# Two stacked graph-attention layers on one core: longer row-sum chains, one head's additions moved to adding transfers, and layer 1's transposes grouped

## The chip, the cores and the metric

The kernel runs on one core of one Trainium2 chip. A core has five engines that run side by side, each with its own queue in strict order: TensorE (PE, matrix products into PSUM; its weight loads are listed as PEld), VectorE (DVE), ScalarE (ACT), GpSimd (POOL) and SyncE (SP, which here only issues transfers). Sixteen DMA engines move data between HBM and SBUF, the on-chip memory. The metric is the device time of one execution in microseconds (us), as the median over runs.

## The reference

The input is x with 8 batches of 2048 nodes and 256 features, and one adjacency matrix adj of 2048 x 2048 for all batches. Two layers follow each other; each adds its result to its input and normalizes every row.

```python
# layer 0: 8 heads of 32 features; the prior is adj itself
x_proj = einsum('bnd,hdf->bhnf', x, W)
e = leaky_relu(e_src[..., :, None] + e_dst[..., None, :], 0.2)
e = e + beta * log(adj + 1e-6)
e = where(adj > 0, e, -inf)
h = softmax(e) @ x_proj
x = layernorm(x + concat_heads(h) @ W_out.T)
# layer 1: one head, dot-product scores
h1, h2, h3 = x @ W1, x @ W2, x @ W3
e = where(adj > 0, leaky_relu(h1 @ h2.T, 0.2), -1e12)
x = layernorm(x + relu(softmax(e) @ h3))
```

All is in 32-bit floating point. In layer 0 a score depends on a source and a destination value only, so the exponential of the score can be written as a product of factors of the row and the column and the larger of two terms; the mask times the prior is one matrix for all batches and heads.

## The kernel before, in words

The kernel is one long program without loops on the chip. Nodes are cut into NT = 16 row tiles of P = 128. Tiles of 128 x 2048 of 32-bit numbers ("wide" tiles) take 8 KB of each partition.

Layer 0 (class `Gat`). Heads go in NP = 4 pairs of HP = 2. One unit of work is one pair and one row tile `jt` (method `step`, 64 units per batch). For each of the two heads, DVE makes a wide tile `s` of unnormalized, transposed attention weights in one instruction (L375): the larger of the column row `c` and a per-partition factor `re`, times the mask matrix's tile `mt`. `mt` comes from DRAM, where batch 0 put it (`load_mt`, L202), into a pool of two buffers. PE then multiplies `s` by the head's values `v` and adds up over the 16 tiles in the PSUM tile `val`; four products, two heads by two halves of the columns, stand side by side in the array, each 32 columns wide (method `products`, L407).

The row sums of the softmax (the denominators) are needed too. For a tile in no chain, PE makes them by a second set of products with the same `s`, into the PSUM tile `den`; the weight operand is then the factor `e`, repeated 32 times. For the tiles of a chain (the table `SUMMED`, by batch and pair) PE leaves these out, and the sum is kept in SBUF, in one wide tile `d` for each head. The first tile of a chain starts `d` by a scaled copy on ACT (L392). Each later tile of the chain is added by one DVE instruction for each head (L386), one unit late: at unit jt the tile jt - 1 is added, after the `s` of unit jt. At the last unit PE multiplies both `d` by a block of ones into `den`, so a chain costs one tile's products at its end. Before the change, the chains hold 6 tiles in three pairs of batch 1; in batches 2 to 7 they hold 4 tiles in the first pair and 8 in each of the others. Batch 0 and the first pair of batch 1 have none.

Layer 1 (class `Dot`). A step takes one row tile: PE multiplies the queries by all keys (L538, four PSUM tiles `e`), ACT applies the leaky ReLU on the way out into the wide tile `p` (L540), DVE masks `p` and finds the row's extreme (L543), and ACT takes the exponential in place (L546). In the next step PE transposes `p` in four groups of four 128 x 128 blocks (function `turned`, L561), ACT copies each group to `pts` (L563), and PE multiplies by `h3` into the PSUM tile `acc` (L577). The last lines divide, add the residual and normalize. In the kernel before, the first group is transposed ahead of the next row tile's scores; the other three stand between the products, each one group ahead.

How the layers meet. For each batch, layer 0 of the next batch is woven into layer 1 of this one: `dot.step` calls `fill` at three places, and each call runs some layer-0 units. The order of PE's instructions is the order of the program text (`manual_schedule` for PE from the start, for SP from batch 1 on); the other engines' orders are set by a scheduler at build time. PSUM is full: `ps` has three buffers of one bank, shared by all short products ("mm" tiles), and `pacc` holds `val`, `den` and `acc`.

SBUF buffers that matter here, by tag: `s` 4, `mt` 2, `d` 2, `c` 3 and `p` 2 wide tiles; `pt` (the `pts`) 2 and `v` 3 small ones. In batch 0 the two `p` buffers also serve the first loads of x and the making of the mask matrix (`make_m`).

Of the kernel before, what the change touches and what calls it, by code (L numbers as in the profile page):

```python
# [27 lines left out]
def kernel(  # L28
# [36 lines left out]
    IG = BK // P  # L65


    SUMMED = [[()] * NP, [()] + [(0, 3, 6, 8, 11, 14)] * (NP - 1)]
    SUMMED += [[(2, 4, 10, 13)] + [tuple(range(0, NT, 2))] * (NP - 1)] * (B - 2)

    const = ctx.enter_context(tc.tile_pool(name="const", bufs=1))
    dram = ctx.enter_context(tc.tile_pool(name="dram", bufs=1, space=DRAM))
    whole = ctx.enter_context(tc.tile_pool(name="whole", bufs=1))
# [48 lines left out]
            nc.vector.tensor_mul(wa, wp[:, kc, 0:D], a_bc)  # L122
            nc.vector.tensor_reduce(dst[:, kc, :], wa.rearrange("p (h f) -> p h f", h=H), AX.X, ALU.add)

    first_x = [wide.tile([P, NT // 2, D], F32, tag="p", name="xr", bufs=2) for _ in range(2)]
    for g in range(NB):
        nc.sync.dma_start(first_x[g // 2][:, ts(g % 2, IG), :],
                          x[0].rearrange("(t p) d -> p t d", p=P)[:, ts(g, IG), :])
# [5 lines left out]
    def later_weights():  # L134

        nc.sync.dma_start(w3s, w3.rearrange("(k p) d -> p k d", p=P))
        w1t, w2t = (chunk.tile([P, KC, D], F32, tag="pt", name=name, bufs=2) for name in ("w1t", "w2t"))
        for w, dst in ((w_out, wot), (w1, w1t), (w2, w2t)):
            src = [row_tile("square") for _ in range(KC)]
            for o in range(KC):  # L140
                nc.sync.dma_start(src[o], w[ts(o, P), :])
            yield
            for kc in range(KC):
                t = mm_tile("sq_t")
                for o in range(KC):
                    nc.tensor.transpose(t[:, ts(o, P)], src[o][:, ts(kc, P)], ident)
                nc.scalar.copy(dst[:, kc, :], t[:, 0:D])
        yield
        for dc in range(KC):
            t = mm_tile("w12p")  # L150
            for kc in range(KC):
                nc.tensor.matmul(t[:, 0:D], w1t[:, kc, ts(dc, P)], w2t[:, kc, :], start=(kc == 0), stop=(kc == KC - 1))
            nc.scalar.copy(w12[:, dc, :], t[:, 0:D])
        yield
# [23 lines left out]
    def make_m(jt):  # L178

        a = wide.tile([P, NT, P], I32, tag="d", name="adj_t", bufs=2)  # L180
        nc.sync.dma_start(a, adj[:, ts(jt, P)].rearrange("(t p) j -> p t j", p=P))
        m = wide.tile([P, NT, P], F32, tag="p", name="m", bufs=2)
        nc.vector.tensor_scalar(m, a, 0.0, None, ALU.max)
        nc.scalar.activation(m, m, AF.Ln, bias=eps_prior)
        nc.scalar.activation(m, m, AF.Exp, scale=beta_c)
        nc.vector.scalar_tensor_tensor(m, a, 0.0, m, ALU.is_gt, ALU.mult)
        return m
# [46 lines left out]
    class Gat:  # L234
# [12 lines left out]
        def scores_first(self, xt):  # L247


            t = mm_tile("scores")  # L250
            for kc in range(KC):
                for q in range(NB):
                    nc.tensor.matmul(t[ts(q, DH), :], wp[:, kc, D:], xt[:, kc, ts(q, BK)],
                                     start=(kc == 0), stop=(kc == KC - 1))
            s = chunk.tile([P, BK], F32, tag="pt", name="scores", bufs=2)
            nc.scalar.copy(s, t)
            t = mm_tile("scores_t")
            for k in range(IG):
                nc.tensor.transpose(t[:, ts(k, P)], s[:, ts(k, P)], ident)
            nc.scalar.copy(self.both.rearrange("p (q k) h -> p k q h", k=IG),  # L260
                           t.rearrange("p (k q h) -> p k q h", k=IG, h=DH)[:, :, :, 0:2 * H])
# [38 lines left out]
            nc.sync.dma_start(c_d[self.b].rearrange("h (t p) -> (h t) p", p=P), est)  # L300

        def load(self, hp):
            self.v[hp] = chunk.tile([P, NT, HP * DH], F32, tag="v", name="v", bufs=3)
            nc.sync.dma_start(self.v[hp], v_d[self.b, hp])

        def load_factors(self):
# [33 lines left out]
        def step(self, count=1):  # L340

            for _ in range(count):
                hp, jt = next(self.units)
                for work in list(self.later):
                    if next(work, self) is self:
                        self.later.remove(work)
                if hp == NP - 1 and jt == 0 and self.b + 1 < B:
                    gats[self.b + 1].load_factors()

                at = self.b * NP + hp + 1  # L350
                if at < B * NP:
                    gat = gats[at // NP]
                    if jt == 4 and gat.b > 0:
                        gat.load(at % NP)
                    elif jt == 12:
                        gat.scale(at % NP)
                if jt == 0:
                    if self.b > 0:
                        self.cs = [self.cs_ahead.pop(0) for _ in range(HP)]
                    else:  # L360
                        self.cs = [self.query_rows(hp * HP + a) for a in range(HP)]
                    self.val = pacc.tile([P, HALF], F32, tag="val", name="val")
                    self.den = pacc.tile([P, HALF], F32, tag="den", name="den")
                first = self.b == 0 and hp == 0
                if first:
                    self.more_mt(jt + 2, jt > 0)
                if self.b > 0:
                    mt = self.mts.pop(0)
                else:
                    mt = self.mts[jt] if first else load_mt(jt, True)  # L370
                s = []
                for a in range(HP):
                    h = hp * HP + a
                    sa = wide_tile("s", "s", 4)
                    nc.vector.scalar_tensor_tensor(sa, self.cs[a], self.re[:, 0, jt, h:h + 1], mt, ALU.max, ALU.mult)  # L375
                    s.append(sa)
                    if self.b > 0 and jt == NT - 1:
                        self.cs_ahead += [c for c in [next(self.c_loads, None)] if c]
                if self.b > 0 and len(self.mts) < (4 if not SUMMED[self.b][hp] and jt < NT - 4 else 2):
                    self.mts += [t for t in [next(self.mt_loads, None)] if t]  # L380
                v, e = self.v[hp], self.re[:, 1]
                heads = [hp * HP + a for a in range(HP)]
                chain = SUMMED[self.b][hp]
                if jt - 1 in chain[1:]:
                    for d, sa, h in zip(self.sums, self.last, heads):
                        nc.vector.scalar_tensor_tensor(d, sa, e[:, jt - 1, h:h + 1], d, ALU.mult, ALU.add)  # L386
                self.last = s
                self.products(self.val, [v[:, jt, ts(a, DH)] for a in range(HP)], s, jt == 0, jt == NT - 1)
                if jt in chain[:1]:
                    self.sums = [wide_tile("d", "d", 2) for _ in heads]  # L390
                    for d, sa, h in zip(self.sums, s, heads):
                        nc.scalar.activation(d, sa, AF.Copy, scale=e[:, jt, h:h + 1])  # L392
                if jt not in chain:
                    self.products(self.den, [e[:, jt, h:h + 1].to_broadcast([P, DH]) for h in heads], s,
                                  jt == min(set(range(NT)) - set(chain)),
                                  not chain and jt == NT - 1)
                if chain and jt == NT - 1:
                    self.products(self.den, [ones] * HP, self.sums, False, True)
                if jt == NT - 1:
                    work = self.finish(hp)  # L400
                    next(work)
                    self.later.append(work)
# [112 lines left out]
    class Dot:  # L515
# [15 lines left out]

        def scores(self, it):
            pen = mask(it, self.b == 0)
            p = wide_tile("p", "p", 2)
            for c in range(NB):
                t = mm_tile("e")
                for kc in range(KC):
# [11 lines left out]
        def step(self, fill=lambda k: None):  # L549
# [8 lines left out]
            def turned(g):  # L558
                t = mm_tile("pt")
                for k in range(IG):  # L560
                    nc.tensor.transpose(t[:, ts(k, P)], p[:, ts(g * IG + k, P)], ident)  # L561
                pt = chunk.tile([P, BK], F32, tag="pt", name="pts", bufs=2)
                nc.scalar.copy(pt, t)  # L563
                return pt

            pt = turned(0)
            if it + 1 < NT:
                if (it + 1) % IG == 0:
                    self.queries((it + 1) // IG)
# [1 line left out]
            fill(1)  # L571
            acc = pacc.tile([P, D], F32, tag="acc", name="acc")
            for g in range(NB):
                now, pt = pt, turned(g + 1) if g + 1 < NB else None
                for k in range(IG):
                    j = g * IG + k
                    nc.tensor.matmul(acc, now[:, ts(k, P)], self.h3[:, j, :], start=(j == 0), stop=(j == NT - 1))  # L577
            fill(2)
            rec = small.tile([P, 1], F32, name="rec1", bufs=2)
            nc.vector.reciprocal(rec, den)  # L580
# [28 lines left out]
    def others():  # L609
# [18 lines left out]
        for n, (gat, g) in enumerate(groups):  # L628
            if g == 0:
                gat.begin()  # L630
            v = chunk.tile([P, NP, IG, HP * DH], F32, tag="v", name="v", bufs=3)
            for k in range(IG):
                gat.row(g * IG + k, xts[n], v[:, :, k, :])
                if k == 1:
# [103 lines left out]
```

The softmax here doesn't subtract the row's maximum and nothing guards it: scores larger than these inputs give would overflow.

## Time and profile before

The median of three runs is 4321.98 us (4317.75 to 4324.15). The profiled execution took 4317.4 us.

| engine | busy us | share | instructions |
|---|---|---|---|
| PE | 4191.7 | 97% | 24640 |
| PE weight loads | 2202.1 | 51% | 24640 |
| DVE | 3704.8 | 86% | 2468 |
| ACT | 1657.5 | 38% | 3019 |
| POOL | 9.5 | 0% | 14 |

| group | count | busy us | mean ns |
|---|---|---|---|
| DVE, score tiles `s` (L375) | 1024 | 2355.5 | 2343 |
| DVE, additions to `d` (L386) | 318 | 738.5 | 2342 |
| PE, values `val` (L407) | 8192 | 1024.5 | 602 |
| PE, denominators `den` of single tiles (L407) | 5216 | 664.1 | 597 |
| PE, layer 1 products `acc` (L577) | 4096 | 955.9 | 381 |
| PE, layer 1 scores `e` (L538) | 2048 | 904.0 | 594 |
| PE, layer 1 transposes `pt` (L561) | 2048 | 317.7 | 278 |
| ACT, starts of `d` (L392) | 54 | 107.9 | 2011 |

How to read it. Busy time is the time in which at least one instruction of the engine or group ran; on PE several run at once, so a mean of one instruction times its count is more than the busy time. A product of 32-bit numbers appears as two records. Some PE records are missing (5216 of 5648 of `den` are there). The transfers moved 843.50 MB, 195 GB/s on average; the largest part are 496 loads of `mt`, 1 MB each. In the steady part of the run one batch takes about 500 us.

### The profile page before, as it was taken

Reading aid. Unit: us, or ns where it says so; the run is one execution under the profiler, and the core shown is the slowest. Engines: PE = TensorE matmul, PEld = TensorE weight load, DVE = VectorE, ACT = ScalarE, POOL = GpSimd, SP = SyncE. Lnnn points to the kernel's source line nnn. Section 1 sums busy time; section 2 is a strip of 40 time slices with the busy share of each in tenths; the row PEclk is TensorE's granted clock in tenths of the full one; section 3 lists DMA queues with packets and bytes.
Section 4 is the critical chain, followed back from the end, with each engine's and each line's share of the span. In section 5 each row is a group of like instructions: output and inputs, shape, how many; then the busy total and the mean of one; then the engine's idle time right before and its main releaser. Section 6 shows DMA issues by size and latency. Waiting matters only on the chain. (4 is left out here: it accounts for less than half of the span.)

```text
span 4317.4 us, 58896 instructions
## 1 busy us (share of the span) xinstructions
PE 4191.7 (97%) x24640; PEld 2202.1 (51%) x24640; DVE 3704.8 (86%) x2468; ACT 1657.5 (38%) x3019; POOL 9.5 (0%) x14
## 2 busy tenths in 40 slices
PE   7999999999999999999999999999999999999999
PEld 5444455454454545544554544555455445545766
DVE  7878888998899989999899998999899998999222
ACT  7522233333333333333343334333333333433554
POOL 0000000000000000000000000000000000000000
PEclk9999999999999999999999999999999999999999
DMA  8979756666555554556555564555545565544211
GB/s 272 308 258 319 273 198 210 225 229 209 184 191 192 201 203 180 179 184 227 187 193 186 189 207 183 192 190 206 202 176 181 186 226 185 198 171 146 81 50 41
DMA packets 267946, 843.50 MB, mean 195 GB/s; under 512 B 32672, under 2 KB 165792, under 8 KB 193952
## 3 DMA queue, kind: packets, MB, share of 16 engines
q1 hardware_dynamic: 232352, 806.17, 53.0%
q10 hardware_dynamic: 35328, 33.56, 2.3%
q8 instruction: 193, 3.16, 0.3%
q14 instruction: 73, 0.60, 0.0%
HBM read 763.76 MB, written 75.37 MB: 194 GB/s over the span
## 5 line engine op out<-in xcount | busy, mean ns | idle before, releaser
L375 DVE SCALAR_TENSOR_TENSOR s<-c,re,mt 128x2048 f32<-128x2048 f32 x1024 | 2355.5, 2343 | 150.3 <-PE den L407 65.6
L407 PE MATMUL val<-s,v 128*32 128x512 f32 x8192 | 1024.5, 602 | 56.7 <-DVE s L375 56.5
L577 PE MATMUL acc<-h,pts 128*128 128x256 f32 x4096 | 955.9, 381 | 18.5 <-ACT pts L563 18.5
L538 PE MATMUL e<-x1t,h 128*128 128x512 f32 x2048 | 904.0, 594 | 4.6 <-ACT pts L563 4.5
L577 PEld LDWEIGHTS acc<-h,pts 128*128 128x128 f32 x4096 | 746.9, 190 | 119.4 <-ACT pts L563 34.2
L386 DVE SCALAR_TENSOR_TENSOR d<-s,re,d 128x2048 f32<-128x2048 f32 x318 | 738.5, 2342 | 0.0
L407 PE MATMUL den<-s,re 128*32 128x512 f32 x5216 | 664.1, 597 | 0.0
L538 PEld LDWEIGHTS e<-x1t,h 128*128 128x128 f32 x2048 | 379.0, 190 | 451.6 <-issue 413.5
L407 PEld LDWEIGHTS val<-s,v 128*32 128x32 f32 x8192 | 245.5, 110 | 675.0 <-issue 519.9
L563 ACT COPY pts<-pt 128x512 f32<-128x512 f32 x512 | 295.4, 582 | 663.5 <-PE pt L561 660.3
L540 ACT ACTIVATE p<-e 128x512 f32<-128x512 f32 x512 | 302.6, 595 | 426.1 <-PE e L538 412.7
L543 DVE CUSTOM_DVE_ANT_0 p<-p,pen 128x2048 f32<-128x2048 f32 x128 | 292.4, 2284 | 198.7 <-ACT p L540 198.6
L407 PEld LDWEIGHTS den<-s,re 128*32 128x32 f32 x5216 | 181.5, 111 | 396.4 <-issue 394.6
L561 PEld LDWEIGHTS pt<-ident,p 128*128 128x128 f32 x2048 | 238.5, 141 | 214.4 <-issue 173.9
L546 ACT ACTIVATE p<-p,neg 128x2048 f32<-128x2048 f32 x128 | 256.7, 2005 | 232.2 <-DVE neg L543 232.2
L561 PE MATMUL pt<-ident,p 128*128 128x128 f32 x2048 | 317.7, 278 | 0.0
L582 ACT ACTIVATE z<-acc,rec 128x256 f32<-128x256 f32 x128 | 60.7, 474 | 391.6 <-PE acc L577 259.4
L583 DVE TENSOR_TENSOR z<-z,x1r 128x256 f32<-128x256 f32 x128 | 53.8, 420 | 142.9 <-ACT z L582 142.8
L392 ACT ACTIVATE d<-s,re 128x2048 f32<-128x2048 f32 x54 | 107.9, 2011 | 80.0 <-PE den L407 66.3
L268 PE MATMUL proj<-wp,xt 128*128 128x272 f32 (+1 forms) x512 | 132.5, 404 | 4.8 <-ACT v L270 3.2
L528 PE MATMUL h1p<-x1t,w 128*128 128x512 f32 x256 | 117.0, 595 | 9.4 <-ACT x1t L503 9.4
L270 ACT COPY v<-proj 128x256 f32<-128x256 f32 x128 | 47.0, 375 | 202.5 <-PE proj L268 197.5
(88 smaller groups left out, 1919.8 us busy)
## 6 DMA issues: line engine op xcount, KB each, us to landing
mt<-mt_d SPq DMA_DIRECT2D x496, 1024.0 KB
c<-c_d SPq DMA_DIRECT2D x64, 1024.0 KB
pen<-pen_d SPq DMA_DIRECT2D x112, 512.0 KB
xg<-in_x_dram SPq DMA_DIRECT2D x60, 512.0 KB
adj_t<-in_adj_dram SPq DMA_DIRECT2D x16, 1024.0 KB
mt_d<-mt SPq DMA_DIRECT2D x16, 1024.0 KB
rb<-rec_d SPq DMA_DIRECT2D x128, 128.0 KB
x_d<-ht ACTq DMA_DIRECT2D x32, 512.0 KB
```

The costliest lines, as they stand in the source:

```text
L268: nc.tensor.matmul(t[:, 0:cols], xt[:, kc, ts(it % IG, P)], wp[:, kc, 0:cols], start=(kc == 0), stop=(kc == KC - 1))
L375: nc.vector.scalar_tensor_tensor(sa, self.cs[a], self.re[:, 0, jt, h:h + 1], mt, ALU.max, ALU.mult)
L386: nc.vector.scalar_tensor_tensor(d, sa, e[:, jt - 1, h:h + 1], d, ALU.mult, ALU.add)
L407: nc.tensor.matmul(dst[ts(q, DH), ts(c, BK)], weights[q % 2], s[q % 2][:, ds(q // 2 * HALF + c * BK, BK)], start=start, stop=stop)
L528: nc.tensor.matmul(t, w12[:, kc, ts(dc, P)], self.x1t[:, kc, ts(g, BK)], start=(kc == 0), stop=(kc == KC - 1))
L538: nc.tensor.matmul(t, self.h1[:, kc, ts(it % IG, P)], self.x1t[:, kc, ts(c, BK)], start=(kc == 0), stop=(kc == KC - 1))
L540: nc.scalar.activation(p[:, ts(c, BK)], t, AF.Prelu, alpha=ALPHA)
L543: nc.vector.tensor_tensor_reduce(p, p, pen, -1.0, FMAX, ALU.add, ALU.min, neg)
L546: nc.scalar.activation(p, p, AF.Exp, bias=neg, scale=-1.0, accum_out=den)
L561: nc.tensor.transpose(t[:, ts(k, P)], p[:, ts(g * IG + k, P)], ident)
L563: nc.scalar.copy(pt, t)
L577: nc.tensor.matmul(acc, now[:, ts(k, P)], self.h3[:, j, :], start=(j == 0), stop=(j == NT - 1))
```

## The change

It has two parts that share memory.

First, the chains get longer: 10 of 16 tiles (0, 1, 3, 4, 6, 7, 9, 10, 12, 14) in the three later pairs of batches 1 to 7, and 6 tiles (2, 4, 6, 8, 10, 12) in the first pair of batches 2 to 7. It is meant to take denominator products off PE. So that DVE needn't make all the additions, those of the pair's first head, for tiles up to BY_DMA = 12, are made otherwise: ACT writes the scaled tile into a wide tile `w` (one buffer), and a transfer issued by GpSimd adds `w` into `d`. The later tile 14, and all of the second head, stay on DVE.

Second, all four transposes of a row tile of layer 1 now stand together at the head of the step, ahead of the next row tile's scores. Then `p` is free before the next scores are written and needs one buffer, which makes room for `w`; the four `pts` need four buffers, which the third buffer of `v` makes room for. The first loads of x and `make_m` use the tags `p` and `w` in turn.

```diff
-    SUMMED = [[()] * NP, [()] + [(0, 3, 6, 8, 11, 14)] * (NP - 1)]
-    SUMMED += [[(2, 4, 10, 13)] + [tuple(range(0, NT, 2))] * (NP - 1)] * (B - 2)
+    SUMMED = [[()] * NP, [()] + [(0, 1, 3, 4, 6, 7, 9, 10, 12, 14)] * (NP - 1)]
+    SUMMED += [[(2, 4, 6, 8, 10, 12)] + [(0, 1, 3, 4, 6, 7, 9, 10, 12, 14)] * (NP - 1)] * (B - 2)
+    BY_DMA = 12
...
-    first_x = [wide.tile([P, NT // 2, D], F32, tag="p", name="xr", bufs=2) for _ in range(2)]
+    first_x = [wide.tile([P, NT // 2, D], F32, tag=tag, name="xr", bufs=1) for tag in "pw"]
...
-        m = wide.tile([P, NT, P], F32, tag="p", name="m", bufs=2)
+        m = wide.tile([P, NT, P], F32, tag="pw"[jt % 2], name="m", bufs=1)
...
-            self.v[hp] = chunk.tile([P, NT, HP * DH], F32, tag="v", name="v", bufs=3)
+            self.v[hp] = chunk.tile([P, NT, HP * DH], F32, tag="v", name="v", bufs=2)
...
                 if jt - 1 in chain[1:]:
                     for d, sa, h in zip(self.sums, self.last, heads):
-                        nc.vector.scalar_tensor_tensor(d, sa, e[:, jt - 1, h:h + 1], d, ALU.mult, ALU.add)
+                        if h == heads[0] and jt - 1 <= BY_DMA:
+                            w = wide_tile("w", "w", 1)
+                            nc.scalar.activation(w, sa, AF.Copy, scale=e[:, jt - 1, h:h + 1])
+                            nc.gpsimd.dma_start(d, w, accum_op=ALU.add)
+                        else:
+                            nc.vector.scalar_tensor_tensor(d, sa, e[:, jt - 1, h:h + 1], d, ALU.mult, ALU.add)
...
-            p = wide_tile("p", "p", 2)
+            p = wide_tile("p", "p", 1)
...
-                pt = chunk.tile([P, BK], F32, tag="pt", name="pts", bufs=2)
+                pt = chunk.tile([P, BK], F32, tag="pt", name="pts", bufs=NB)
...
-            pt = turned(0)
+            pts = [turned(g) for g in range(NB)]
...
-                now, pt = pt, turned(g + 1) if g + 1 < NB else None
                 for k in range(IG):
                     j = g * IG + k
-                    nc.tensor.matmul(acc, now[:, ts(k, P)], self.h3[:, j, :], start=(j == 0), stop=(j == NT - 1))
+                    nc.tensor.matmul(acc, pts[g][:, ts(k, P)], self.h3[:, j, :], start=(j == 0), stop=(j == NT - 1))
```

More of the change, by code (lines that the diff above doesn't have):

```diff
@@ L136, in later_weights @@
         nc.sync.dma_start(w3s, w3.rearrange("(k p) d -> p k d", p=P))
-        w1t, w2t = (chunk.tile([P, KC, D], F32, tag="pt", name=name, bufs=2) for name in ("w1t", "w2t"))
+        w1t, w2t = (chunk.tile([P, KC, D], F32, tag="pt", name=name, bufs=NB) for name in ("w1t", "w2t"))
         for w, dst in ((w_out, wot), (w1, w1t), (w2, w2t)):
@@ L254, in scores_first @@
                                      start=(kc == 0), stop=(kc == KC - 1))
-            s = chunk.tile([P, BK], F32, tag="pt", name="scores", bufs=2)
+            s = chunk.tile([P, BK], F32, tag="pt", name="scores", bufs=NB)
             nc.scalar.copy(s, t)
@@ L630, in others @@
                 gat.begin()
-            v = chunk.tile([P, NP, IG, HP * DH], F32, tag="v", name="v", bufs=3)
+            v = chunk.tile([P, NP, IG, HP * DH], F32, tag="v", name="v", bufs=2)
             for k in range(IG):
```

## The prediction

> **What bounds the kernel now.** I read first the busy shares of the engines over the whole span and in its 40 slices, then a steady stretch of four batches in windows of 500 us, then the groups by line and the timeline of one row-tile step, and last the table of waits.
>
> ```profile
> PE 4191.7 (97%) x24640; PEld 2202.1 (51%) x24640; DVE 3704.8 (86%) x2468; ACT 1657.5 (38%) x3019; POOL 9.5 (0%) x14
> ...
> PE   7999999999999999999999999999999999999999
> ...
> DVE  7878888998899989999899998999899998999222
> ACT  7522233333333333333343334333333333433554
> ...
> DMA  8979756666555554556555564555545565544211
> ...
> q1 hardware_dynamic: 232352, 806.17, 53.0%
> ```
>
> TensorE is the fullest engine in every slice after the first, VectorE is close behind until the last batch's layer 1 stands alone (the last three slices), ScalarE has more than half its time free, GpSimd does nothing, and the 16 DMA engines are a little over half busy. The windows of the steady part say the same with numbers (columns: stretch, its length, busy time of PE, weight loads, DVE, ACT, POOL, then clock, DMA share and GB/s):
>
> ```profile
> 1650.00:2150.00 500.00, 489.04 (x2870) 250.40 (x2870) 467.23 (x304) 185.49 (x324) 0.00 (x0) 1.00 0.55 194
> 2150.00:2650.00 500.00, 487.82 (x2860) 249.00 (x2859) 466.03 (x302) 182.95 (x321) 0.00 (x0) 1.00 0.55 194
> 2650.00:3150.00 500.00, 488.75 (x2863) 250.61 (x2865) 466.92 (x304) 185.18 (x323) 0.00 (x0) 1.00 0.55 193
> ```
>
> In the steady part PE is 98% busy, DVE 93%, ACT 37%, DMA 55%. One batch is 128 score-tile instructions of L375, and the trace places the first of each batch 503 us after that of the batch before (502 in batch 1). So work taken off PE shortens the kernel only while DVE, which has 7% left, and the new DMA traffic stay below it.
>
> ```profile
> L375 DVE SCALAR_TENSOR_TENSOR s<-c,re,mt 128x2048 f32<-128x2048 f32 x1024 | 2355.5, 2343 | 150.3 <-PE den L407 65.6
> ...
> L386 DVE SCALAR_TENSOR_TENSOR d<-s,re,d 128x2048 f32<-128x2048 f32 x318 | 738.5, 2342 | 0.0
> L407 PE MATMUL den<-s,re 128*32 128x512 f32 x5216 | 664.1, 597 | 0.0
> ...
> L392 ACT ACTIVATE d<-s,re 128x2048 f32<-128x2048 f32 x54 | 107.9, 2011 | 80.0 <-PE den L407 66.3
> ```
>
> and from the timeline of one step (start, length, what):
>
> ```profile
> 2000.13 3.64 PE L407 MATMUL val<-s,v 128*32 128x512 f32 x32
> ...
> 2004.02 0.13 PEld L407 LDWEIGHTS den<-s,re 128*32 128x32 f32 x4 [0.30 <-issue]
> 2004.45 0.13 PEld L407 LDWEIGHTS den<-s,re 128*32 128x32 f32 x4 [0.30 <-issue]
> ```
>
> These are the prices: one addition on DVE 2.342 us, the same pass on ACT 2.011 us, and one row tile's denominator products on PE. The last: a tile makes 16 records in four groups; groups of loads follow each other at 2004.45 - 2004.02 = 0.43 us, so 4 x 0.43 = 1.72 us of PE. (664.1 / 5216 x 16 = 2.04 us by busy time, which counts the pipeline's tails.) I use 1.72, the flow rate, and keep 2.04 as the upper end.
>
> ```profile
> PE val L407 <- DVE s L375: 56.5, 47, 3.3
> DVE s L375 <- DMA mt<-mt_d: 54.7, 25, 5.6
> ...
> PE acc L577 <- ACT pts L563: 18.5, 36, 1.3
> ```
>
> (engine, line, what it waited for: us in total, times, longest.) The waits that PE has are small: 57 us for score tiles, 19 for evicted transposes. DVE waits 55 us in all for mask rows `mt`; today those loads are hidden.
>
> **What the Trainium skill says.** "DMA: Bandwidth & Descriptors", section SWDGE vs HWDGE vs iDMA: a transfer that adds into its destination can only be issued from GpSimd. The trace of before has no such transfer. The same page, Anatomy of one DMA: a GpSimd transfer carries about 2 us of fixed cost beside its data. No row of before shows it. "Collectives: The Full Stack", section The bandwidth ceiling: an add in the DMA costs no time of its own, but reads two sources per byte written, and the measured rate halves. That is my price for the new transfer. "SBUF — State Buffer", section Who interferes with whom: only VectorE's two-port modes lock GpSimd out of writing descriptors, and the two-tensor operations are not among them; VectorE's long operations here (L375, L386) are of that kind, so I expect no starvation of the new queue, which the trace of before cannot confirm.
>
> **The change, part by part.**
>
> Row tiles taken from PE. Batch 1: three pairs go from 6 to 10 chained tiles, 3 x 4 = 12. Batches 2 to 7: the first pair goes from 4 to 6, the others from 8 to 10, so 2 x 4 = 8 each, 48 in all. 60 tiles x 1.72 = 103 us off PE (122 at 2.04). These lie in the stretches where PE is 98% busy, so they lie on the path.
>
> DVE additions. Before 318. After, head 0 of a pair is added by transfer for tiles up to 12. A 10-chain then has 8 transfers, 1 DVE addition for head 0 (tile 14) and 9 for head 1; the 6-chain has 5 and 5. DVE: batch 1 keeps 30; each later batch has 5 + 30 = 35 instead of 48. In all 240, 78 fewer, 78 x 2.342 = 183 us, or 30 us of each later batch's 470 (93% of 503). DVE then needs 440 of about 489, 90%: not the bound, and a little more forgiving than now.
>
> ScalarE. Each transfer needs its scaled copy `w`, one 2.011 us pass: batch 1 has 24, the later ones 5 + 24 = 29 each, 198 in all, 398 us. ACT goes from 37% to about 50% of the steady part: free by sum. By place: in the built order one `w` stands behind the four `pts` copies and before the four evictions of the next scores, another behind the exponential. Four transposes take about 0.6 us of PE and their copy 0.58 us on ACT; a score tile takes PE 1.7 us (four groups of 0.43), and with three PSUM buffers the fourth, 5.1 us on, needs the first evicted. ACT, done with the copies 0.6 us into the scores, runs `w` to 2.6 and the first eviction (0.595, L540) to 3.2: covered, with 1.9 us to spare. Past that it would hold the score evictions, then PE.
>
> DMA. 806.17 MB took 53.0% of 4317 us: 2.84 us of all 16 engines per MB, 2.98 us per 128x2048 tile. The new transfer at the least costs one such copy, 2.98; at twice the reads 5.95, which I take; at three times (read, read and write not overlapping) 8.9. A later batch has now 0.545 x 503 = 274 us of DMA; plus 29 transfers: 360 (74% of 489), 447 (91%), or 532, which is more than the batch. It stops fitting at (489 - 274) / 29 = 7.4 us.
>
> New waits. `w` has one buffer, so ACT's next `w` waits until the transfer has landed (5.95 + 2 = about 8 us), with everything queued behind it on ACT. The unit (one row tile of one pair) lasts 489 / 64 = 7.6 us on average; tiles 3-4, 6-7 and 9-10 are neighbours, 3 places in each of 21 pairs, 63 in all. Eight us against 7.6 plus the 1.9 us of cover: mostly nothing. The `mt` loads share the DMA engines with the adds; a load that meets one takes up to twice as long and has two buffers. I charge 20 us in all for both, between 0 and 60; a guess bounded by the 55 us that such loads cost today.
>
> Layer 1's transposes together, and one `p` buffer. The same 16 transposes and 16 products; weight loads run back to back in both orders, so PE time is equal. The 19 us of waits for `pts` should go. Against it: four transposes fill three PSUM buffers, so PE needs ACT's first copy within about a microsecond. I set these off against each other, 0, within +/- 20. One `p` suffices as all transposes now stand ahead of the next scores in PE's order. Four `pts`, `v` with two buffers and the split `p`/`w` tags: nothing; `v` could make batch 0's projections wait for a store a few times (under 10 us).
>
> Sum: 4322 - 103 + 20 = 4239 us.
>
> **Rivals.** (1) The latencies take it all back: ACT waits for the landing at the 63 neighbours and PE with it. 1.5 us each gives 95 us: 4322 - 103 + 95 = 4314, no change. For it: the single buffer and ACT's strict order; against: ACT is half idle and PSUM gives 1.9 us of cover. (2) The DMA engines become the bound, at 8.9 us per transfer: 532 instead of 503 us in six batches, +175, and in batch 1 0.61 x 502 = 306 plus 24 x 8.9 = 520, +18: 4322 + 193 = 4515, slower. For it: no row of before shows an adding transfer, and 7.4 us is only 1.25 times my price; against: the first slices show these engines at 0.9 with the kernel running well. (3) DVE, having less to do, stops being the second limit, and PE's waits for score tiles also halve: 4322 - 122 - 28 = 4172. It needs a load that is never late.
>
> **How the numbers follow.** Forecast 0.64, with rival 3 inside its lower tail another 0.04; rival 1 0.13; rival 2 0.19. The time is the forecast's, 4239. The range reaches down to 4185 (103 at its upper end 122, no new waits, some relief) and up to 4360, past rival 1 and short of rival 2, leaving out rival 2 and little else. 0.2% is 8.6 us: rival 1 spreads over 4280 to 4350, so 0.04 of it counts as faster, 0.06 as same, 0.03 as slower. Faster 0.72, same 0.06, slower 0.22.
>
> **What would show it.** Right: the `den` group smaller by a sixth, DVE's additions 240, ACT some 400 us fuller, DMA share near 0.85 to 0.9 in the steady windows, PE still at 97 to 98%, batches near 489 us. Wrong: PE busy down but span not, with PE or DVE waiting on ACT's `pts` or `p` behind `w` (rival 1), or DMA at 0.95 and DVE's wait for `mt` in the hundreds (rival 2). The price of the adding transfer is what would most easily make the prediction wrong.

## The result, and the profile after

The changed kernel takes 4595.89 us (median of 4 runs, 4584.86 to 4604.65) against 4321.67 us of the kernel before: a ratio of 1.0634, 95% interval 1.0608 to 1.0661. It is 274 us slower, where 83 us less was forecast; the time is above the range.

The page of the kernel after (its lines stand one to seven further down in the file: L376 is now the score tiles `s`, L390 the new `w`, L393 the DVE additions, L414 the products of `val` and `den`):

```profile
PE 4221.2 (92%) x23680; PEld 2225.0 (49%) x23680; DVE 3552.6 (78%) x2390; ACT 2013.4 (44%) x3217; POOL 181.7 (4%) x212
...
q1 hardware_dynamic: 232352, 806.17, 50.9%
q0 software_dynamic: 28512, 207.63, 22.4%
...
L390 ACT ACTIVATE w<-s,re 128x2048 f32<-128x2048 f32 x198 | 397.3, 2007 | 563.5 <-DMA d<-w 367.3
...
L393 DVE SCALAR_TENSOR_TENSOR d<-s,re,d 128x2048 f32<-128x2048 f32 x240 | 561.6, 2345 | 12.1 <-ACT d L399 11.0
L414 PE MATMUL den<-s,re 128*32 128x512 f32 x4256 | 546.8, 596 | 0.0
...
d<-w POOLq DMA_DIRECT2D x198, 1024.0 KB, 11.2
```

The work moved as the change meant it to. The `den` group fell by 664.1 - 546.8 = 117 us and from 5216 to 4256 records, which are the 60 row tiles at 16 records each. (No record of `den` is missing before, as was said above: the 432 others are the products with `d`.) DVE makes 240 additions, ACT is 356 us fuller. The last line is new: an adding transfer lands 11.2 us after its issue (median). The steady windows show no engine full:

```profile
1650.00:2150.00 500.00, 461.86 (x2566) 241.73 (x2561) 409.49 (x268) 224.81 (x330) 23.24 (x27) 0.97 0.79 235
2150.00:2650.00 500.00, 462.46 (x2531) 234.66 (x2527) 410.93 (x267) 223.32 (x331) 23.20 (x27) 0.96 0.80 237
```

PE 92%, DVE 82%, ACT 45%, DMA 80%, and PE's granted clock 0.96 to 0.97 where it was 1.00. So the time went into waits. The table of waits (us in total, times, longest), in part:

```profile
ACT w L390 <- DMA d<-w: 367.3, 81, 13.4
...
PE pt L568 <- ACT pts L570: 117.8, 44, 7.7
DVE s L376 <- DMA mt<-mt_d: 111.4, 49, 5.4
PE val L414 <- DVE s L376: 94.1, 67, 5.3
...
PE e L545 <- ACT p L547: 49.7, 16, 4.7
```

ACT stood 81 times until the adding transfer before had landed, 4.5 us each on average. Only ACT, and GpSimd's queue with it, waited for the landing of an adding transfer, so the sum `d` was not late for those who read it. Summed over all of PE's instructions, ACT ended 246 us of PE's idle time (51 before) and DVE 96 us (57 before). One place where ACT stood, in the timeline:

```profile
2286.23 2.05 ACT L570 COPY pts<-pt 128x512 f32<-128x512 f32 x4 [1.22 <-PE pt L568]
...
2287.36 5.41 PE L545 MATMUL e<-x1t,h 128*128 128x512 f32 x12
...
2291.32 0.19 PEld L545 LDWEIGHTS e<-x1t,h 128*128 128x128 f32 x1 [0.24 <-issue]
2291.75 0.19 PEld L545 LDWEIGHTS e<-x1t,h 128*128 128x128 f32 x1 [0.24 <-issue]
2293.00 2.35 DVE L393 SCALAR_TENSOR_TENSOR d<-s,re,d 128x2048 f32<-128x2048 f32 x1
2293.33 2.00 ACT L390 ACTIVATE w<-s,re 128x2048 f32<-128x2048 f32 x1 [5.05 <-DMA d<-w]
2295.24 1.55 ACT L547 ACTIVATE p<-e 128x512 f32<-128x512 f32 x3
...
2295.87 3.57 PE L545 MATMUL e<-x1t,h 128*128 128x512 f32 x4 [3.10 <-ACT p L547]
2296.89 0.34 PEld L545 LDWEIGHTS e<-x1t,h 128*128 128x128 f32 x1 [0.52 <-issue]
2297.74 0.34 PEld L545 LDWEIGHTS e<-x1t,h 128*128 128x128 f32 x1 [0.52 <-issue]
```

ACT finishes the four `pts` copies at 2288.3 and then waits 5.05 us for the landing of the last `w`, makes the next one, and only then empties the scores. PE has filled its three PSUM buffers (12 records are three score tiles) and stands for 3.10 us. And PE loses more than that: before the gap its loads follow at 0.43 us, after it at 0.85. Windows over the two stretches show why (the third column from the right is the clock):

```profile
2287.40:2292.40 5.00, 5.00 (x14) 2.15 (x12) 5.00 (x3) 0.88 (x2) 0.00 (x0) 1.00 0.99 256
2295.90:2299.30 3.40, 3.40 (x4) 1.14 (x4) 0.00 (x0) 0.89 (x2) 0.58 (x1) 0.53 1.05 325
```

After the gap PE runs at half clock for some 3.4 us. The trace's clock records have 62 such stretches (59 of them of 3.41 or 6.83 us) where the kernel before has 12. Of the 62, 57 start in a PE gap of 2 us or more or within 9 us after it.

The sum comes near. PE's idle time is the span less its busy time: 4583.0 - 4221.2 = 361.8 us, 236 more than before (4317.4 - 4191.7 = 125.7). Time at half clock was 293 us, before 52. Of these, 44 and 5 us fell in PE's gaps, where a low clock costs nothing more; half of the rest is lost, 124 and 23 us, so 101 more. With 103 us of products removed: 236 + 101 - 103 = 234, against 266 between the two profiled executions. The other 32 us are not accounted for.

### The profile page after: what moved, and what is told of

It reads as the page before. It is cut to its first block, busy times and chain, and to the rows that moved or that the text cites. A ratio compares the mean times of both kernels' runs of the same rounds, so it can differ in the third digit from the quotient of the medians.

```text
span 4583.0 us, 57477 instructions
## 1 busy us (share of the span) xinstructions
PE 4221.2 (92%) x23680; PEld 2225.0 (49%) x23680; DVE 3552.6 (78%) x2390; ACT 2013.4 (44%) x3217; POOL 181.7 (4%) x212
## 3 DMA queue, kind: packets, MB, share of 16 engines
q1 hardware_dynamic: 232352, 806.17, 50.9%
q0 software_dynamic: 28512, 207.63, 22.4%
## 5 line engine op out<-in xcount | busy, mean ns | idle before, releaser
L376 DVE SCALAR_TENSOR_TENSOR s<-c,re,mt 128x2048 f32<-128x2048 f32 x1024 | 2356.7, 2346 | 248.1 <-DMA mt<-mt_d 111.4
L414 PE MATMUL val<-s,v 128*32 128x512 f32 x8192 | 1055.6, 613 | 99.1 <-DVE s L376 94.1
L545 PE MATMUL e<-x1t,h 128*128 128x512 f32 x2048 | 967.7, 626 | 85.1 <-ACT p L547 49.7
L583 PE MATMUL acc<-h,pts 128*128 128x256 f32 x4096 | 915.1, 381 | 0.0
L390 ACT ACTIVATE w<-s,re 128x2048 f32<-128x2048 f32 x198 | 397.3, 2007 | 563.5 <-DMA d<-w 367.3
L414 PEld LDWEIGHTS val<-s,v 128*32 128x32 f32 x8192 | 248.5, 111 | 759.3 <-issue 530.7
L393 DVE SCALAR_TENSOR_TENSOR d<-s,re,d 128x2048 f32<-128x2048 f32 x240 | 561.6, 2345 | 12.1 <-ACT d L399 11.0
L414 PE MATMUL den<-s,re 128*32 128x512 f32 x4256 | 546.8, 596 | 0.0
L568 PE MATMUL pt<-ident,p 128*128 128x128 f32 x2048 | 272.8, 283 | 129.7 <-ACT pts L570 117.8
L570 ACT COPY pts<-pt 128x512 f32<-128x512 f32 x512 | 268.3, 594 | 159.3 <-PE pt L568 155.8
L391 POOL DMA_DIRECT2D d<-w x198 | 171.3, 865 | 3582.3 <-ACT w L390 2919.6
L414 PEld LDWEIGHTS den<-s,re 128*32 128x32 f32 x4256 | 152.3, 111 | 320.1 <-issue 312.1
## 6 DMA issues: line engine op xcount, KB each, us to landing
d<-w POOLq DMA_DIRECT2D x198, 1024.0 KB, 11.2
```

The source lines that it names most:

```text
L390: nc.scalar.activation(w, sa, AF.Copy, scale=e[:, jt - 1, h:h + 1])
L414: nc.tensor.matmul(dst[ts(q, DH), ts(c, BK)], weights[q % 2], s[q % 2][:, ds(q // 2 * HALF + c * BK, BK)], start=start, stop=stop)
L545: nc.tensor.matmul(t, self.h1[:, kc, ts(it % IG, P)], self.x1t[:, kc, ts(c, BK)], start=(kc == 0), stop=(kc == KC - 1))
L583: nc.tensor.matmul(acc, pts[g][:, ts(k, P)], self.h3[:, j, :], start=(j == 0), stop=(j == NT - 1))
```

## The experiments

Three theories were set against each other. A: ACT, held until an adding transfer has landed, starves PE. B: layer 1's grouped transposes make PE depend on ACT. C: the DMA traffic of the adds delays the mask rows, and so DVE and PE. Each time stands beside runs of the kernel before on the same chip (4318 to 4320).

**Layer 1's transposes grouped, nothing else.** The kernel after with

```diff
-    SUMMED = [[()] * NP, [()] + [(0, 1, 3, 4, 6, 7, 9, 10, 12, 14)] * (NP - 1)]
-    SUMMED += [[(2, 4, 6, 8, 10, 12)] + [(0, 1, 3, 4, 6, 7, 9, 10, 12, 14)] * (NP - 1)] * (B - 2)
-    BY_DMA = 12
+    SUMMED = [[()] * NP, [()] + [(0, 3, 6, 8, 11, 14)] * (NP - 1)]
+    SUMMED += [[(2, 4, 10, 13)] + [tuple(range(0, NT, 2))] * (NP - 1)] * (B - 2)
+    BY_DMA = -1
```

> The chains of the kernel before, all additions on DVE, no adding transfer; layer 1's transposes grouped and the buffers as in the kernel after. Theory A (ACT is held until the last adding transfer has landed, 11.2 us in the profile after, and PE stands idle behind it and loses clock): 4300 to 4345, no change to before, PE clock 0.99. Theory B (the grouped transposes with one p make PE wait for ACT): above 4450, with PE's waits for pts over 80 us as in the profile after (118). Theory C (the traffic of the adding transfers delays the mask rows): as A.

Measured: 4363.67 us, ratio 1.0105 (1.0090 to 1.0120). That is 44 us slower, a little outside what A allowed and far from B. The place comes once in each of the batches 1 to 7, where a pair ends and the next chain starts. In the timeline of this run:

```profile
2252.62 1.53 PE L568 MATMUL pt<-ident,p 128*128 128x128 f32 x12
2252.70 1.02 ACT L430 COPY dn<-den 128x1024 f32<-128x1024 f32 x1 [0.76 <-PE val L414]
2253.61 3.89 ACT L399 ACTIVATE d<-s,re 128x2048 f32<-128x2048 f32 x2
...
2257.40 1.54 ACT L570 COPY pts<-pt 128x512 f32<-128x512 f32 x3
...
2258.03 1.11 PE L568 MATMUL pt<-ident,p 128*128 128x128 f32 x4 [3.88 <-ACT pts L570]
```

Behind the first three groups PE waits 3.88 us for a PSUM buffer, as ACT first makes the two starts of the next chain. The fourth group then takes 1.11 us instead of some 0.6: half clock again. In the kernel before only the first group stood here, and the scores behind it had two free buffers; PE waited 0.70 us. The table of this run:

```profile
PE pt L568 <- ACT pts L570: 33.2, 21, 3.9
```

Seven of these 21 waits, one in each batch, are of 3.0 to 3.9 us and make up 25 us; about 15 us more than before are lost to half clock. Together they come near the 44.

**The same with two `p` buffers**, to tell the grouping from the single buffer:

```diff
-            p = wide_tile("p", "p", 1)
+            p = wide_tile("p", "p", 2)
```

(with `first_x` and `m` back on two buffers of tag `p`).

> The run with the grouped transposes alone (4364), but with two p buffers as in the kernel before (there is room without w); v 2 and pts 4 stay. If the grouping itself costs the 44 us (PE needs ACT's copies within a microsecond and starts the scores later): 4355 to 4370. If the single p costs them: 4315 to 4330.

Measured: 4364.21 us, 1.0105 (1.0090 to 1.0120). The grouping itself costs the 44 us; the single `p` costs nothing that can be seen.

**No transfers.** The kernel after without the line of the adding transfer:

```diff
-                            nc.gpsimd.dma_start(d, w, accum_op=ALU.add)
```

> The kernel after without the adding transfers: ACT still makes every w, but nothing adds it, so head 0's row sums lack those tiles. No traffic and no landing. Theory A: 4210 to 4250, 70 to 110 below before, the 103 us of PE work that the longer chains save. Theory B: still above 4450. Theory C: 4210 to 4250 too.

Measured: 4287.56 us, 0.9926 (0.9911 to 0.9941), below before but less so than expected; the 44 us of the grouping are in it. So the longer chains with `w` on ACT are worth 4364 - 4288 = 76 us, and everything that the 198 transfers do costs 4596 - 4288 = 308 us. B is out as the main cause; A and C are left. PE's waits of this run, which the table above has at 117.8 and 94.1 us with the transfers:

```profile
PE val L413 <- DVE s L376: 66.8, 48, 3.0
...
PE pt L567 <- ACT pts L569: 29.7, 21, 3.1
```

Over all instructions ACT ends 81 us of PE's idle time here and DVE 68. So with the transfers ACT adds 165 us and DVE 28. That puts A well ahead of C, but it tells who ended a wait, and not what had made ACT or DVE late.

**No two transfers at neighbouring units.**

```diff
-    BY_DMA = 12
+    BY_DMA = (1, 4, 7, 10, 12)
...
-                        if h == heads[0] and jt - 1 <= BY_DMA:
+                        if h == heads[0] and jt - 1 in BY_DMA:
```

> The kernel after, but only tiles 1, 4, 7, 10 and 12 of a chain go by transfer, so that no two stand at neighbouring units; 3, 6 and 9 go to DVE. 120 transfers instead of 198, 318 DVE additions, as many as before; PE does the products of the kernel after. Theory A: ACT's wait for landings falls from 367 us to under 40, PE's clock is back at 0.99, time 4240 to 4300, below before. Theory B: still above 4450. Theory C: in between, about in proportion to the transfers, 4450 to 4500.

Measured: 4416.73 us, 1.0221 (1.0205 to 1.0236), with 123 transfers (the first pairs' 4, 10 and 12 are among them) and 315 DVE additions. ACT's wait for landings is gone from the table, as A said, and 179 of the 274 us came back, but the time is not below before: A alone is not enough. The clock is at 0.985, DVE's wait for mask rows has grown (before 54.7), and batch 1 alone takes 540 us (before 502):

```profile
DVE s L376 <- DMA mt<-mt_d: 102.5, 52, 5.4
```

The 129 us over the run without transfers need not all be traffic: DVE makes 75 more additions here and is 91% busy in the steady windows. This run doesn't part the two. Landing still takes 11.2 us, so it is no queue behind a neighbouring add; what else makes it longer is not settled.

**Adds that read another source.** Meant to keep the traffic and take ACT's wait away:

```diff
-                            nc.gpsimd.dma_start(d, w, accum_op=ALU.add)
+                            seen = small.tile([P, 1], F32, name="seen", bufs=2)
+                            nc.gpsimd.tensor_copy(seen, w[:, 0:1])
+                            nc.gpsimd.dma_start(d, mt_d[ts(jt - 1, P), :], accum_op=ALU.add)
```

> The kernel after with all 198 adding transfers at their places and of their size, but each reads a row of the mask matrix in DRAM instead of w (the row sums are then wrong in value), after a small GpSimd copy that reads one column of w. So ACT's next w waits for that copy and not for the landing. Traffic stays, ACT's wait goes. Theory A: 4210 to 4290. Theory B: above 4450. Theory C: above 4450, DVE waiting over 100 us for mask rows.

Measured: 4770.60 us, 1.1052 (1.1033 to 1.1070). It doesn't tell the theories apart, for it did not take the wait away:

```profile
POOL d L393 <- DMA d<-mt_d: 1605.9, 170, 14.4
...
ACT w L390 <- POOL seen L392: 522.8, 56, 21.1
```

The small copy stands in GpSimd's queue behind transfers that wait for earlier landings, so ACT was held longer than before, now through GpSimd. More holding came with more time, which speaks for A no more than loosely.

**`w` in two halves**, each with its own buffer and transfer, the bytes unchanged:

```diff
-                            w = wide_tile("w", "w", 1)
-                            nc.scalar.activation(w, sa, AF.Copy, scale=e[:, jt - 1, h:h + 1])
-                            nc.gpsimd.dma_start(d, w, accum_op=ALU.add)
+                            for k in range(2):
+                                w = wide.tile([P, HALF], F32, tag="w", name="w", bufs=2)
+                                nc.scalar.activation(w, sa[:, ts(k, HALF)], AF.Copy, scale=e[:, jt - 1, h:h + 1])
+                                nc.gpsimd.dma_start(d[:, ts(k, HALF)], w, accum_op=ALU.add)
```

(`first_x` and `m` in halves to match, here and in the next.)

> The kernel after, but each w is made and added in two halves of 1024 columns, each half with a buffer, a pass on ACT and a transfer of its own (396 transfers of 512 KB). ACT then needs only the first half of the last w landed before it can go on, some 3 to 5 us earlier. Theory A (of the 308 us between this kernel without and with its transfers, most is ACT held until the landing): 4400 to 4520. Theory C (most is the DMA traffic, which delays mask rows and so DVE and PE): 4570 to 4640, no gain.

Measured: 4455.04 us, 1.0322 (1.0303 to 1.0340). 141 us of the time return:

```profile
q0 software_dynamic: 57024, 207.64, 26.1%
...
ACT w L400 <- DMA d<-w: 204.6, 84, 6.7
```

ACT's wait for landings falls from 367 to 205 us, although the transfers now take more of the DMA (26.1% of the span instead of 22.4%). C, which expected no gain, can't explain that.

**`w` in bf16 with two buffers**, the sum still in 32 bits:

```diff
-                            w = wide_tile("w", "w", 1)
+                            w = wide_tile("w", "w", 2, BF16)
```

> The kernel after with w in bf16, so that two buffers of it fit where one was; the transfer reads half the bytes and adds into the 32-bit sum. ACT's next w waits for the landing of the last but one, which is past. Theory A: ACT's wait for landings under 60 us, 4300 to 4370. Theory C: 4450 to 4560, the traffic still being most of what it was.

Measured: 4367.35 us, 1.0111 (1.0095 to 1.0127), 229 us below the kernel after. ACT no longer waits for a landing anywhere in the table, though a landing still takes 10.7 us: it is the single buffer, not the length as such, that hurt. But the transfers also take less of the DMA than the 22.4% of the kernel after, so not all of the 229 us is the buffer's:

```profile
q0 software_dynamic: 28512, 207.63, 18.0%
```

The clock is back at 0.987.

**Traffic without any wait of ACT.** In place of the adding transfer, after each `w` (`from_d` and `to_d` are buffers in DRAM of 1 MB each):

```diff
-                            nc.gpsimd.dma_start(d, w, accum_op=ALU.add)
+                            seen = small.tile([P, 1], F32, name="seen", bufs=2)
+                            nc.gpsimd.tensor_copy(seen, w[:, 0:1])
+                            k = Gat.count % 4
+                            Gat.count += 1
+                            nc.gpsimd.dma_start(from_d[k][0:1, 0:1], seen[0:1, :])
+                            nc.gpsimd.dma_start(to_d[2 * k], from_d[k])
+                            nc.gpsimd.dma_start(to_d[2 * k + 1], from_d[k])
```

> As the kernel without transfers (4288), plus traffic that nobody waits for: after each w a small GpSimd copy of one column, a one-element transfer, and two plain DRAM to DRAM copies of 1 MB each, about the DMA time of one adding transfer. Head 0's row sums lack the tiles of the transfers. Theory A: 4290 to 4340. Theory C: 4450 or more, DVE waiting over 100 us for mask rows.

Measured: 4443.98 us, 1.0292 (1.0276 to 1.0308), between the two. These copies take 24.5% of the span on the DMA engines (the adds took 22.4%) and, unlike the adds, load HBM on both sides (377 GB/s in all, 183 in the kernel after), so I take their 156 us over the run without transfers as an upper bound for the traffic of the adds; that such copies disturb the other loads at least as much as adds within SBUF is argued, not shown. The delay runs as C has it:

```profile
DVE s L382 <- DMA mt<-mt_d: 135.0, 68, 8.2
PE val L426 <- DVE s L382: 124.8, 84, 6.2
```

**All additions on DVE.** The kernel before with the longer chains only (the `SUMMED` of the change, nothing else).

> The kernel before with the longer chains of the kernel after and nothing else: all additions on DVE (438 instead of 318), no w, no transfer. If DVE becomes the bound, as its 93% in the steady part says: 16 more additions per later batch make 470 + 37 = 507 us of DVE in a batch that lasts 503, so 4400 to 4550 with PE waiting for score tiles some hundreds of us. If PE's products still set the time: near 4220.

Measured: 4481.42 us, 1.0378 (1.0361 to 1.0395). DVE becomes the bound: 96% busy in the steady windows, batches of 526 us, and PE waits for it:

```profile
1650.00:2150.00 500.00, 471.56 (x2602) 239.50 (x2600) 483.14 (x311) 178.54 (x316) 0.00 (x0) 0.97 0.51 180
...
PE val L407 <- DVE s L375: 198.5, 116, 6.2
```

So the change was right that the longer chains' additions can't all go to DVE.

**Few, spaced transfers on the kernel before.** The interleaved transposes and the old chains of batch 1 and of the first pairs stay; `v` gives up a buffer for a bf16 `w` of 4 KB:

```diff
-    SUMMED += [[(2, 4, 10, 13)] + [tuple(range(0, NT, 2))] * (NP - 1)] * (B - 2)
+    SUMMED += [[(2, 4, 10, 13)] + [(0, 1, 3, 4, 6, 7, 9, 10, 12, 14)] * (NP - 1)] * (B - 2)
+    BY_DMA = (1, 4, 7, 10, 12)
...
-                        nc.vector.scalar_tensor_tensor(d, sa, e[:, jt - 1, h:h + 1], d, ALU.mult, ALU.add)
+                        if self.b > 1 and hp > 0 and h == heads[0] and jt - 1 in BY_DMA:
+                            w = wide_tile("w", "w", 1, BF16)
+                            nc.scalar.activation(w, sa, AF.Copy, scale=e[:, jt - 1, h:h + 1])
+                            nc.gpsimd.dma_start(d, w, accum_op=ALU.add)
+                        else:
+                            nc.vector.scalar_tensor_tensor(d, sa, e[:, jt - 1, h:h + 1], d, ALU.mult, ALU.add)
```

> The kernel before with its interleaved transposes and its chains in the first pair and in batch 1; in the 18 other pairs the chain of ten tiles, with head 0's tiles 1, 4, 7, 10 and 12 by transfer from a single bf16 w (4 KB, room from v at two buffers). 36 row tiles or 62 us off PE, DVE as before, 90 transfers. If ACT is never held and the traffic costs little: 4265 to 4300, below both kernels. If a transfer costs by its traffic, about 1 us each as in the run with spaced transfers: 4330 to 4360.

Measured: 4290.50 us, 0.9932 (0.9914 to 0.9950): 0.7% faster than the kernel before, and faster than both. PE is at 96 to 97% in the steady windows, the DMA at 68%, the clock at 0.99 to 1.00:

```profile
2150.00:2650.00 500.00, 481.57 (x2792) 249.00 (x2788) 463.32 (x303) 213.60 (x340) 12.89 (x15) 1.00 0.68 226
```

Of the 62 us of products removed some 29 arrive; where the other 33 go was not looked into.

**The same with batch 1 too:**

```diff
-    SUMMED = [[()] * NP, [()] + [(0, 3, 6, 8, 11, 14)] * (NP - 1)]
+    SUMMED = [[()] * NP, [()] + [(0, 1, 3, 4, 7, 9, 10, 12)] * (NP - 1)]
...
-                        if self.b > 1 and hp > 0 and h == heads[0] and jt - 1 in BY_DMA:
+                        if self.b > 0 and hp > 0 and h == heads[0] and jt - 1 in BY_DMA:
```

> The run with few bf16 transfers (4290), with batch 1's three later pairs at a chain of eight tiles too (0, 1, 3, 4, 7, 9, 10, 12) with tiles 1, 4, 7, 10 and 12 of head 0 by transfer: 6 more row tiles or 10 us off PE, 3 fewer DVE additions, 15 more transfers. If a spaced transfer costs next to nothing: 4275 to 4287. If batch 1, whose DMA share is higher than that of the later ones, can't take the traffic: 4290 to 4310.

Measured: 4323.26 us, 1.0011 (1.0004 to 1.0018), worse than both guesses. Batch 1 goes from 501 to 531 us, the later batches are unchanged. Its DMA share rises from 0.63 to 0.71, and more waits of several kinds appear (for the adjacency tiles of the mask, 22 us instead of 2, for `mt`, 19 instead of 14, for `pts`, 15 instead of 5). Which of them leads is not settled.

## Why the prediction was wrong, step by step

- **What bounds the kernel**: right. PE was the bound with DVE close behind; the run with all additions on DVE hits DVE at once.
- **Row tiles taken from PE**, 103 us (122 at the upper end): right, 117 us less busy time in the group; without the transfers 76 us of it reached the time. **DVE additions**: 240, right. **ScalarE**: 198 passes, 397 us, right. None of them was the trouble.
- **DMA**: the price of an adding transfer was close. 22.4% of 4583 us over 198 is 5.2 us of all 16 engines, against the 5.95 that I had estimated from the halved rate for adds in the Trainium skill, "Collectives: The Full Stack", section The bandwidth ceiling. That page was thus a good guide to throughput. The DMA share is 0.80, below the 0.91 I worked out, in good part because a batch lasts some 540 us and not 489. So rival 2, the DMA engines as the bound, did not happen; of its signs only DVE's wait for `mt`, 111 us, came. Nor was the new queue starved by VectorE: an issue took GpSimd 0.85 to 1.37 us.
- **New waits**: this is the step that failed. "Eight us against 7.6 plus the 1.9 us of cover: mostly nothing" took the landing as engine time plus the fixed 2 us that the Trainium skill gives in "DMA: Bandwidth & Descriptors", section Anatomy of one DMA, as if the transfer had the engines to itself. The shortest landing, 6.9 us, is about that sum; the median is 11.2 us. It also counted from the wrong point: the buffer is taken when ACT starts to write `w`, 2.3 us ahead of the issue, so it is free again 13.5 us after that start. And an average unit of 7.6 us says little, for the units are not evenly spaced. In the run without transfers 104 of the 197 distances from one `w` to the next are under 13.5 us, and 14 are under 6. The result was 81 waits of 4.5 us on ACT, 367 us, where I had priced 20 us in all. Rival 1 named the mechanism, and mis-sized it: 95 us, no change.
- **Missing altogether**: that an idle PE comes back at half clock. It turns 236 us of more idle time into some 337 us of loss. On average, every wait I priced should have been dearer by four tenths: (236 + 101) / 236 = 1.4.
- **Layer 1's transposes**, "0, within +/- 20": wrong by 44 us. I had written that PE now needs ACT's first copy within about a microsecond, and didn't look up what ACT has queued ahead of it where a pair ends and a chain starts: 5 us of evictions and chain starts. The 19 us of waits for `pts` that I wanted to save came back as 33.
- **Traffic**: I charged it with the waits, 20 us for both. DVE's wait for `mt` alone rose by 57 us, from 54.7 to 111.4. Two runs give a size: 79 us for all that the transfers cost with two bf16 buffers and half the bytes read, 156 us for plain copies through HBM.

Together: +44 for the grouping, -76 for the longer chains, and +308 for the transfers, 276 in all against 4320. If the two sizes bound the traffic, which is not shown, ACT's hold is the other 152 to 229 of the 308. That both can act is shown, A by the halves and C by the plain copies, for traffic of about this size. That A is about half of the transfers' cost or more is shown by the halves alone: 141 of 308 us came back at no less traffic, with 205 us of waits still there. The split is not settled beyond that, as no run kept the exact traffic of the adds with ACT wholly free. Why batch 1 bears transfers so badly is open too.

## What to carry to other kernels

Before a transfer's result or its source buffer is put in the way of an engine that also empties PSUM, compare the time from the first write to the landing, not its share of the DMA, with the shortest distance between two uses, and give the source a second buffer first. Count a gap on TensorE as more than its length: here the gaps cost about four tenths more on average, at half clock. And when a step is moved to just behind another engine's short copies, look at what that engine's queue holds ahead of them at the irregular places, here where a pair ends and a chain starts.

## What the runs showed of the hardware

- An adding transfer of 1 MB within SBUF landed 11.2 us after issue (6.9 to 14.9), the same when spaced; 10.7 us (5.7 to 13.6) with a bf16 source; each half of 512 KB 8.6 us (4.5 to 15.0). It took 5.2 us of the 16 engines, 4.0 us with the bf16 source (18.0% of 4362.3 us over 198), where the same bytes on the queue of the plain transfers beside it took 3.0 (50.9% of 4583 us over 806.17 MB, at 1.049 MB each). Its issue took GpSimd 0.86 us.
- With PE gaps the granted clock fell to 0.5, mostly for 3.41 or 6.83 us: 12 such stretches in the kernel before, 62 after. In the kernel after, a stretch started in the gap or within 9 us after it for all 34 gaps over 3.4 us, for 23 of 28 between 2 and 3.4 us, for 21 of 60 between 1 and 2 us, and for 2 of 32 between 0.5 and 1 us.
